# Which queue issues the loads and stores of a spectral layer: tokens to SyncE's queue, the second batch's stores to GpSimd's queue

## The chip, the cores and the metric

The kernel runs on one core of a Trainium2 chip. The metric is the device time of one launch in microseconds (us). The time before is the median of three runs.

## The reference, cut to what matters

The input is an image batch of 2 x 128 x 64 x 64, that is two batches of 4096 positions with 128 channels. It goes through a convolutional attention layer, through a plain self-attention over the positions, and then through the layer that this change is about, a spectral one:

```python
def _stu_conv(phi, u, n):
    sgn = jnp.where(jnp.arange(sl) % 2 == 0, 1.0, -1.0)
    Vf = jnp.fft.rfft(phi, n=n, axis=0)
    Uf_p = jnp.fft.rfft(u, n=n, axis=1)
    Uf_m = jnp.fft.rfft(u * sgn3, n=n, axis=1)
    U_plus = jnp.fft.irfft(Vf[None, :, :, None] * Uf_p[:, :, None, :], n=n, axis=1)[:, :sl]
    U_minus = jnp.fft.irfft(Vf[None, :, :, None] * Uf_m[:, :, None, :], n=n, axis=1)[:, :sl]
    return (U_plus, U_minus * sgn[None, :, None, None])
...
out = jnp.einsum('btkd,k,kde->bte', U_plus, s, Mpp)
out = out + jnp.einsum('btkd,k,kde->bte', U_minus, s, Mpm)
...
return _compute_spectral(u, sigma, phi, Mpp, Mpm) + _compute_ar_u(Mu, u)
```

So 16 causal filters of length 4096 are convolved with every channel, each result is mixed by a 128 x 128 matrix, and a short convolution of three taps (`_compute_ar_u`) is added. The layer's output is added to its own input.

## The kernel before

One launch does everything, in this order: the first attention (lines 193 to 482), the self-attention of batch 0 and then of batch 1 (`attend`, lines 1008 to 1121), and the spectral layer (from line 1274). The program is built by a recording layer that keeps the order of the code on each engine and on each queue.

**What is prepared.** `filters16` writes the transformed filters as "tables" to DRAM. `feed(b)` (lines 1123 to 1212) normalises a batch, transforms it (`pf`, line 1160), splits the result into two float16 parts (`uh`, lines 1132 and 1133) and stores them to DRAM as "rows" (lines 1166, 1167 and 1199). For each of its eight blocks of 512 positions it issues eight stores of 64 KB, in pieces of 256 bytes. Its inner function `taps` computes the three taps plus the layer's input and stores this as "base" (line 1148, 256 KB each), from the single buffer `oc`, which ScalarE writes at line 1140. `feed(0)` runs beside the self-attention of batch 1. `feed(1)` runs beside the first quarter of the spectral layer, as the iterator `beside`.

**The spectral layer's loop.** It runs over batch `b`, output row parity `ro`, eight chunks `ch` and two input streams `s`: 64 steps. In the text a pass is one pair (`b`, `ro`), that is 16 steps, and a half is half a step. For each half, `chunk16` (lines 1300 to 1323) issues two loads of "tokens", 128 KB each, the same rows into partitions 0 to 63 and 64 to 127 (line 1309), and one load of a table, 1024 KB (line 1314). Both kinds of tile have two sets of buffers, so the loads for a half are issued when the convolution of the same half two steps earlier has read its buffers. `convolve16` then multiplies tokens by table on TensorE (`cv`, line 1372; eight matmuls in a half), ScalarE and VectorE split the result into `x` (lines 1379 and 1380), and `mix16` does 48 matmuls for a step (`m`, line 1388).

The two access patterns that matter here, of a token load and of a table load, have different outermost dimensions on the DRAM side: 4 x 16 rows of 2 KB for tokens, 8 x 16 overlapping windows of 8 KB for a table.

`back` (lines 1454 to 1520) turns a finished pass back to positions, four blocks at a time, beside the next pass. `turned` loads the base part of the block into the single buffer `had` (line 1484, 256 KB), and `inverse` adds it (line 1502). After the last pass `back` uses other buffers (`added`, line 1475).

**Queues.** A DMA is issued by an engine, and an engine issues in order: a DMA that waits for data or for a free buffer holds up everything behind it on the same queue. Before the change, SyncE's queue (SP) issues, in the order in which the loop reaches them, the tables of the whole layer, the stores of both feeds, the base stores, the `had` loads, and the four token loads of step 0. GpSimd's queue (POOL) issues the token loads of steps 1 to 63, 252 in all, and has nothing else to do in this stage apart from one memset and some short powers.

Of the kernel before, what the change touches and what calls it, by code (L numbers as in the profile page):

```python
# [38 lines left out]
BP = NI // 2  # L39
# [36 lines left out]
def conv_attn_hybrid(ctx: ExitStack, tc: tile.TileContext, io):  # L76
    nc = tc.nc
# [31 lines left out]
    def pool(stack, name, bufs=1, **kw):  # L109
        return stack.enter_context(tc.tile_pool(name=name, bufs=bufs, reuse_waits="tile", **kw))  # L110
# [599 lines left out]
    base = [dram.tile([C, NI, P], F32, name=f"base{b}") for b in range(B)]  # L710
# [45 lines left out]

    def layers(st, layer0, in_halves):
        psum_a = st.enter_context(ExitStack())

        tokens = [pool(st, f"tok{b}", side="right") for b in range(B)]  # L760
        tok = [tokens[b].tile([P, NI, C], F32, tag="t", name=f"tok{b}") for b in range(B)]
# [360 lines left out]

        def feed(b, p, bank, fw, stats=None):


            if stats is None:
                stats = LayerStats(p, tok[b], f"f{b}")
                yield from stats.steps()
            to = rows16[b].rearrange("h c r w d -> w c h r d") if in_halves else rows[b].rearrange("c r w d -> w c r d")

            def parts(dst, pf):
                nc.scalar.activation(dst[:, 0], pf, AF.Copy, scale=U_SCALE)
                nc.vector.scalar_tensor_tensor(dst[:, 1], pf, U_SCALE, dst[:, 0], ALU.mult, ALU.subtract)

            def taps(i, uT):
                oc = p.tile([P, 4, P], F32, tag="oc", name=f"oc{b}_{i}", bufs=1)
                pt = bank(f"tT{b}_{i}").rearrange("p (t c) -> p t c", c=C)
                for t in range(4):
                    nc.tensor.transpose(pt[:, t, :], tok[b][:, 4 * i + t, :], ident)
                nc.scalar.copy(oc, pt)  # L1140
                yield
                pa = bank(f"ar{b}_{i}").rearrange("p (t c) -> p t c", c=C)
                for n in range(NU):
                    nc.tensor.matmul(pa, mu[:, n, :], uT[:, 2 - n : 6 - n, :], start=(n == 0), stop=(n == NU - 1))  # L1144
                    if n == 0:
                        yield
                nc.vector.tensor_tensor(oc, pa, oc, ALU.add)
                nc.sync.dma_start(base[b][:, 4 * i : 4 * i + 4, :], oc)
                yield

            before = first = None
            for i in range(NQ):
                un = p.tile([P, 4, C], F32, tag="un", name=f"un{b}_{i}")
                for t in range(4):
                    stats.normed(un[:, t, :], 4 * i + t)
                yield
                for c in range(2):
                    at = BP + 1 + 2 * i
                    pf = bank(f"pf{b}_{i}_{c}").rearrange("p (t c) -> p t c", c=C)
                    nc.tensor.matmul(pf, fw[:, c, :], un, start=True, stop=True)  # L1160
                    if in_halves:
                        uh = p.tile([P, 2, 4, C], F16, tag="uh", name=f"uh{b}_{i}_{c}")
                        uhr = uh.rearrange("w h (p r) d -> w h p r d", r=2)
                        parts(uh, pf)
                        for h in range(2):
                            nc.sync.dma_start(to[:, c, h, 2 * i : 2 * i + 2, :], uhr[:, h, :, 0, :])
                            nc.sync.dma_start(to[:, c, h, at : at + 2, :], uhr[:, h, :, 1, :])
                    else:
                        uh = p.tile([P, 4, C], F32, tag="uh", name=f"uh{b}_{i}_{c}")
                        uhr = uh.rearrange("w (p r) d -> w p r d", r=2)  # L1170
                        nc.scalar.copy(uh, pf)
                        nc.sync.dma_start(to[:, c, 2 * i : 2 * i + 2, :], uhr[:, :, 0, :])
                        nc.sync.dma_start(to[:, c, at : at + 2, :], uhr[:, :, 1, :])
                    yield

                uT = p.tile([P, 6, P], F32, tag="uT0" if i == 0 else "uT", name=f"uT{b}_{i}", bufs=1 if i == 0 else 2)
                pt = bank(f"uT{b}_{i}").rearrange("p (t c) -> p t c", c=C)
                for t in range(4):
                    nc.tensor.transpose(pt[:, t, :], un[:, t, :], ident)
                nc.vector.tensor_tensor(uT[:, 2:, :], pt, mask.unsqueeze(1).to_broadcast([P, 4, P]), ALU.mult)  # L1180
                if i:
                    nc.vector.tensor_copy(uT[:, :2, :], before[:, 4:, :])
                    yield
                    yield from taps(i, uT)
                else:
                    first = uT
                    yield
                before = uT
            ul = p.tile([P, 2, 2, C], F16, tag="ul", name=f"ul{b}", bufs=1) if in_halves else p.tile([P, 2, C], F32, tag="ul", name=f"ul{b}", bufs=1)
            for c in range(2):  # L1190
                pf = bank(f"pl{b}_{c}")[:, :C]
                nc.tensor.matmul(pf, fw[:, 2 + c, :], un[:, 3, :], start=True, stop=True)
                if in_halves:
                    parts(ul[:, c], pf)
                else:
                    nc.scalar.copy(ul[:, c, :], pf)
            if in_halves:
                for c in range(2):
                    nc.sync.dma_start(to[:, c, :, BP, :], ul[:, c])
            else:  # L1200
                nc.sync.dma_start(to[:, :, BP, :], ul)
            yield

            nc.gpsimd.memset(first[:, :2, 0:1], 0.0)
            nc.vector.tensor_tensor(
                first[:, :2, 1:],
                before[:, 4:, : P - 1],
                mask[:, 1:].unsqueeze(1).to_broadcast([P, 2, P - 1]),
                ALU.mult,
            )  # L1210
            yield
            yield from taps(0, first)
# [78 lines left out]
        def ordered(instruction):  # L1291
            return tc.keep_in_program_order(instruction)

        def one_bank(name):
            return pc.tile([P, 512], F32, tag="bk", name=name)
# [4 lines left out]
        def chunk16(n, b, ro, ch, s):  # L1300

            row = FIRST[STREAM[ro, s]]
            halves = []
            for half in range(2):
                w0 = 2 * NS * ch + NS * half
                tt = tables_in[n % 2][half]
                ut = tokens_in[n % 2][half]
                for copy in range(2):
                    (nc.gpsimd if n else nc.sync).dma_start(  # L1309
                        ut[64 * copy : 64 * copy + 64],  # L1310
                        rows16[b].rearrange("h c r w d -> (h c) r w d")[:, row : row + BP, w0 : w0 + NS, :],
                    )
                own = tables16[s, w0 // NS]
                nc.sync.dma_start(
                    tt,
                    bass.AP(
                        tensor=own.tensor,
                        offset=own.offset,
                        ap=[[NDI * NS * 2 * NK, 8], [NS * 2 * NK, BP], [1, BP * NS * 2 * NK]],
                    ),  # L1320
                )
                halves.append((tt, ut))
            return halves
# [130 lines left out]
        def back(b, ro, oh, outs, p):  # L1454
# [3 lines left out]
            baser = base[b].rearrange("c (q r) j -> c r q j", r=2)  # L1458
# [18 lines left out]
            def turned(p4):  # L1477

                u = f"{b}_{ro}_{p4}"
                if end:  # L1480
                    had, v = ends[p4][0], ends[p4][1].rearrange("p (c q) x -> p c q x", c=2)
                else:
                    had = p.tile([P, 4, P], F32, tag="had", name=f"had{u}", bufs=1)
                    nc.sync.dma_start(had, baser[:, ro, 4 * p4 : 4 * p4 + 4, :])
                    v = p.tile([P, 2, 4, C], F32, tag="v", name=f"v{u}", bufs=1)
                for c in range(2):
                    pt = pc.tile([P, 512], F32, tag="cv", name=f"vt{u}_{c}", bufs=3) if end else one_bank(f"vt{u}_{c}")
                    pt = pt.rearrange("p (q c) -> p q c", c=C)
                    for q in range(4):
                        ordered(nc.tensor.transpose(pt[:, q, :], ohr[:, c, BP - 1 - 4 * p4 - q, :], ident))  # L1490
                    (nc.scalar.copy if c else nc.vector.tensor_copy)(v[:, c, :, :], pt)
                    yield had, v
# [201 lines left out]
```

## Time and profile before

| what | value |
|---|---|
| time, median of 3 runs | 2817.92 us (2805.27 to 2823.38) |
| the profiled execution | 2826.95 us, of which 2824.8 us are the span of its instructions |
| TensorE busy (PE) | 2686.4 us, 95% of the span |
| VectorE (DVE), ScalarE (ACT), GpSimd (POOL) busy | 1717.3, 1908.9 and 310.7 us |
| spectral layer's loop, first `cv` matmul to last `x` | 1757.9 to 2790.7 us of the span |
| tables, q1 (queue of SP) | 128 loads of 1024 KB |
| tokens, q0 (queue of POOL) | 252 loads of 128 KB, 14.5 us from issue to landing in the median |

How it is read: times in the profile are counted from the start of the span. A row of the view by windows gives a stretch of the span, its length, the busy time of each engine in it with the number of instructions, the mean TensorE clock that was granted (PEclk, 1.00 is full), the mean busy share of the core's 16 DMA engines, and the rate that they moved. A row of the view of waits reads: who waited, for what, how many us in total, how often, and the longest. The chain of waits follows the end of the program back through what released each piece of work. "SPq" and "POOLq" are the queues of SyncE and GpSimd.

### The profile page before, as it was taken

The page shows a single profiled execution, that of the slowest core. Times are in us where ns is not written, and L with a number is a line of the kernel's source. Part 1 is how long each engine was busy: PE and PEld are TensorE (multiplying, and loading weights), DVE is VectorE, ACT ScalarE, POOL GpSimd, SP SyncE. Part 2 cuts the span into 40 slices and gives each one's busy share as a digit, 9 for nine tenths or more (in the row PEclk, how much of TensorE's full clock was granted, in tenths as well). Part 3 has the DMA queues.
Part 4 walks back from the last instruction along what each step waited for, and adds up shares of the span by engine and source line. Part 5 has one row for each costly group of instructions (what it writes and reads, how often), then busy time and mean ns, then how long its engine had stood idle before and what let it go on. Part 6 is the DMA issues. An engine that isn't in the chain of part 4 may idle for free.

```text
span 2824.8 us, 34747 instructions
## 1 busy us (share of the span) xinstructions
PE 2686.4 (95%) x12851; PEld 1365.7 (48%) x12851; DVE 1717.3 (61%) x2994; ACT 1908.9 (68%) x2507; POOL 310.7 (11%) x542
## 2 busy tenths in 40 slices
PE   5999999999999999998899999788989999999998
PEld 3555555555445555554455554343444445445444
DVE  5256564256245249779986677565656666666664
ACT  4999999999999976665555565344444554555553
POOL 2022121013010001000100000111111111111110
PEclk9999999999999999999999999899999999999999
DMA  4122120022000013303121100666666566566662
GB/s 142 34 64 81 49 64 22 5 65 63 6 5 7 5 38 42 59 1 105 38 60 38 36 1 14 141 155 159 169 168 177 192 181 189 174 205 177 164 199 94
DMA packets 215635, 253.31 MB, mean 90 GB/s; under 512 B 140720, under 2 KB 171840, under 8 KB 199072
## 3 DMA queue, kind: packets, MB, share of 16 engines
q1 hardware_dynamic: 168128, 197.35, 24.2%
q0 software_dynamic: 44336, 50.44, 7.8%
q10 hardware_dynamic: 2992, 3.22, 0.3%
q8 instruction: 103, 1.69, 0.3%
q14 instruction: 76, 0.62, 0.1%
HBM read 210.50 MB, written 23.33 MB: 83 GB/s over the span
## 4 chain that ended last, share of the span: by engine, by line
PE 45%; DMA 9%; DVE 7%; ACT 1%; issue 1%; SPq 0%; ACTq 0%; DVEq 0%
PE m L1388 18%; PE oacc L1053 9%; PE cv L1372 6%; DMA tables_b<-tables 5%; PE y L1023 5%; PE eT L1043 3%; DMA base<-oc 2%; PE ar L1144 1%; DMA had<-base 1%; DVE x L1380 1%; DVE ep L1085 1%; PE bk L1500 1%; DVE eT L1046 1%; DMA tables_a<-tables 1%; PE pf L1160 1%
## 5 line engine op out<-in xcount | busy, mean ns | idle before, releaser
L464 ACT ACTIVATE e<-s 128x1536 f16<-128x1536 f32 (+1 forms) x704 | 937.1, 1430 | 33.5 <-PE s L208 28.5
L1380 DVE TENSOR_TENSOR x<-cv,x 128x1024 f16<-128x1024 f32 x512 | 602.8, 1219 | 306.0 <-ACT x L1379 305.9
L1379 ACT CAST x<-cv 128x1024 f16<-128x1024 f32 x512 | 493.7, 1017 | 414.0 <-PE cv L1372 413.1
L1388 PE MATMUL m<-x,mxr 128*128 128x512 f16 x2048 | 624.2, 381 | 0.0
L208 PE MATMUL s<-qs,ks 128*128 128x512 f16 x2048 | 558.3, 380 | 7.5 <-ACT e L464 3.8
L208 PE MATMUL acc<-e,v 128*97 128x512 f16 x2048 | 557.6, 379 | 3.4 <-DVE accs L412 0.2
L1388 PE MATMUL m<-x,mxl 128*128 128x512 f16 x1024 | 392.3, 383 | 3.2 <-DVE oh L1395 3.2
L208 PEld LDWEIGHTS <-v 128*97 128x97 bf16 x2048 | 254.8, 125 | 214.9 <-issue 12.9
L1388 PEld LDWEIGHTS <-mxr 128*128 128x128 f16 x2048 | 201.7, 98 | 244.0 <-issue 7.1
L1032 ACT ACTIVATE ey<-y,nshift 128x512 f32<-128x512 f32 x288 | 195.4, 688 | 179.9 <-PE y L1023 140.5
L208 PEld LDWEIGHTS <-ks 128*128 128x128 f16 x2048 | 200.6, 99 | 228.0 <-issue 44.3
L1309 POOL DMA_DIRECT2D tokens<-rows x252 | 153.0, 611 | 852.0 <-PE cv L1372 819.1
L1023 PE MATMUL y<-bothT 128*128 128x512 f16 x864 | 221.9, 380 | 0.6 <-ACT ey L1032 0.5
L1046 DVE TENSOR_TENSOR eT<-eT,eT 128x512 f16<-128x512 f32 x224 | 147.3, 685 | 93.4 <-ACT eT L1045 91.9
L412 DVE COPY accs<-acc 97x512 f32<-97x512 f32 x64 | 44.2, 691 | 262.2 <-PE acc L208 262.1
L1053 PE MATMUL oacc<-ep,hi 128*128 128x512 f16 x576 | 190.8, 380 | 10.5 <-DVE ep L1085 8.1
L1085 DVE TENSOR_TENSOR ep<-ey,ep 128x512 f16<-128x512 f32 x288 | 192.2, 686 | 6.9 <-ACT ep L1084 0.9
L1372 PEld LDWEIGHTS <-tokens 128*128 128x128 f16 x1024 | 100.4, 99 | 167.4 <-issue 69.9
L1045 ACT ACTIVATE eT<-eT 128x512 f16<-128x512 f32 x224 | 132.6, 602 | 70.1 <-PE eT L1043 69.7
L1388 PEld LDWEIGHTS <-mxl 128*128 128x128 f16 x1024 | 101.1, 99 | 132.8 <-DVE oh L1395 10.6
L1053 PEld LDWEIGHTS <-hi 128*128 128x128 f16 x1024 | 100.5, 98 | 130.2 <-issue 16.8
L1372 PE MATMUL cv<-tables_b,tokens 128*128 128x512 f16 x512 | 135.2, 387 | 23.3 <-DMA tables_b<-tables 21.0
(210 smaller groups left out, 2582.5 us busy)
## 6 DMA issues: line engine op xcount, KB each, us to landing
tables_a<-tables SPq DMA_DIRECT2D x64, 1024.0 KB
tables_b<-tables SPq DMA_DIRECT2D x64, 1024.0 KB
tokens<-rows POOLq DMA_DIRECT2D x252, 128.0 KB, 14.5
tab<-in_rot SPq DMA_DIRECT2D x32, 512.0 KB
rows<-uh SPq DMA_DIRECT2D x128, 64.0 KB
ks<-term POOLq DMA_DIRECT2D x112, 64.0 KB, 2.2
qs<-term POOLq DMA_DIRECT2D x112, 64.0 KB, 2.1
accs<-back SPq DMA_DIRECT2D x32, 128.0 KB
```

The costliest lines, as they stand in the source:

```text
L208: tc.keep_in_program_order(nc.tensor.matmul(*args, **kw))
L464: nc.scalar.activation(e[:, own, :], ps[:, own, :], AF.Exp, scale=SCORE_SCALE)
L1023: nc.tensor.matmul(ps[:, q, :], a[0][:, bass.ts(t, P)], c[0][:, bass.ts(i, 512)], start=(n == 0), stop=(n == 2),)
L1032: nc.scalar.activation(e[:, 2 * h + q, :], ps[:, q, :], AF.Exp, bias=nshift16 if in_halves else nshift, accum_out=den[:, t, i : i + 1],)
L1046: nc.vector.tensor_tensor(eT[1], pt, eT[0], ALU.subtract)
L1053: nc.tensor.matmul(acc, a[0][:, own], c, start=(start and t == 0 and n == 0), stop=(stop and t == len(es) - 1 and n == 2),)
L1085: nc.vector.tensor_tensor(es[t][1], e[:, t, :], es[t][0], ALU.subtract)
L1309: (nc.gpsimd if n else nc.sync).dma_start(ut[64 * copy : 64 * copy + 64], rows16[b].rearrange("h c r w d -> (h c) r w d")[:, row : row + B ...
L1372: ordered(nc.tensor.matmul(pu[:, h, :], ut[:, at, :], tt[:, :, at, :], start=True, stop=True))
L1379: nc.scalar.copy(hi, pur)
L1380: nc.vector.tensor_tensor(lo, pur, hi, ALU.subtract)
L1388: nc.tensor.matmul(acc, m, x, start=(s == 0 and i == 0), stop=(s == 1 and i == len(products) - 1))
```

## The change

The token loads of all steps go to SyncE's queue. The rows and base stores of `feed(1)`, 64 + 2 + 8 in all, and the twelve `had` loads go to GpSimd's queue. `feed(0)` stays on SyncE's queue. The order of the instructions on TensorE, VectorE and ScalarE is the same as before; buffers, sizes and access patterns are the same. After it, SyncE's queue holds in this stage, for each half, two token loads and then one table load, and towards the end the base loads at line 1475 and half of the output.

```diff
@@ def layers
         psum_a = st.enter_context(ExitStack())
+        aside = nc.gpsimd if in_halves else nc.sync
...
@@ def feed(b, p, bank, fw, stats=None)
+            queue = aside if b else nc.sync
...
-                nc.sync.dma_start(base[b][:, 4 * i : 4 * i + 4, :], oc)
+                queue.dma_start(base[b][:, 4 * i : 4 * i + 4, :], oc)
...
-                            nc.sync.dma_start(to[:, c, h, 2 * i : 2 * i + 2, :], uhr[:, h, :, 0, :])
-                            nc.sync.dma_start(to[:, c, h, at : at + 2, :], uhr[:, h, :, 1, :])
+                            queue.dma_start(to[:, c, h, 2 * i : 2 * i + 2, :], uhr[:, h, :, 0, :])
+                            queue.dma_start(to[:, c, h, at : at + 2, :], uhr[:, h, :, 1, :])
...
-                    nc.sync.dma_start(to[:, c, :, BP, :], ul[:, c])
+                    queue.dma_start(to[:, c, :, BP, :], ul[:, c])
...
@@ def chunk16(n, b, ro, ch, s)
-                    (nc.gpsimd if n else nc.sync).dma_start(
+                    nc.sync.dma_start(
                         ut[64 * copy : 64 * copy + 64],
...
@@ def back / turned(p4)
-                    nc.sync.dma_start(had, baser[:, ro, 4 * p4 : 4 * p4 + 4, :])
+                    aside.dma_start(had, baser[:, ro, 4 * p4 : 4 * p4 + 4, :])
```

`in_halves` is true on the path that runs; the same edits in the other path (single precision) are not executed.

## The prediction

> **What bounds the kernel now.** I read the stage first. The spectral loop has four passes of 32 halves. The view by windows, cut where each pass starts its first `cv` matmul, shows where TensorE is short of work. Columns: stretch, length, busy PE, PEld, DVE, ACT and POOL with counts, granted clock, DMA share, GB/s.
>
> ```profile
> 1757.90:2071.30 313.40, 268.24 (x1127) 120.84 (x1125) 187.79 (x219) 137.90 (x157) 39.94 (x65) 0.93 0.63 154
> 2071.30:2310.60 239.30, 233.95 (x1121) 111.85 (x1120) 159.63 (x141) 127.22 (x136) 38.79 (x64) 0.99 0.61 185
> 2310.60:2555.30 244.70, 236.64 (x1124) 112.20 (x1123) 161.01 (x154) 127.43 (x136) 38.78 (x64) 0.99 0.63 186
> 2555.30:2790.70 235.40, 232.39 (x1122) 111.43 (x1121) 160.03 (x141) 127.23 (x136) 33.94 (x56) 1.00 0.57 167
> ```
>
> TensorE bounds passes 2 to 4: 703 of 719.4 us busy. In pass 1, beside which `feed(1)` runs, it idles for 313.4 - 268.2 = 45.2 us, at a clock of 0.93. The chain of waits, in the window of pass 1, says why (start, us, what):
>
> ```profile
> 1757.12 22.75 DMA tables_b<-tables
> ...
> 1792.25 19.03 DMA rows<-uh
> ...
> 1835.26 28.97 DMA tables_b<-tables
> ...
> 1869.71 23.60 DMA base<-oc
> ...
> 1903.62 32.19 DMA tables_b<-tables
> ```
>
> A store of 64 or 256 KB takes as long as a table, because both stand on SP's queue, and tables are issued late behind stores. This is what the change takes away. The queues' shares decide what it costs. The DMA view gives packets, MB and share of 16 engines; these are its q1 (SP) and q0 (POOL) lines for pass 1, passes 2 to 4, and for 2154 to 2300, an even stretch of pass 2:
>
> ```profile
> q1 hardware_dynamic: 23644, 39.98, 49.9%
> ```
>
> ```profile
> q1 hardware_dynamic: 19213, 102.71, 44.3%
> ```
>
> ```profile
> q1 hardware_dynamic: 2911, 22.36, 44.5%
> q0 software_dynamic: 5998, 5.67, 16.1%
> ```
>
> Last, windows of a few us in which one kind of transfer runs. The first three hold the four token loads that SP issues already (issue 1562.5 to 1564.7); the fourth, a base store; the last two, tables alone, with two outstanding:
>
> ```profile
> 1564.00:1566.00 2.00, 2.00 (x12) 0.95 (x10) 1.91 (x4) 1.31 (x5) 0.00 (x0) 1.00 0.22 75
> 1566.00:1568.00 2.00, 2.00 (x7) 0.83 (x7) 1.97 (x4) 0.94 (x2) 0.00 (x0) 1.00 0.26 99
> 1568.00:1569.50 1.50, 1.50 (x9) 0.68 (x8) 0.73 (x2) 0.00 (x0) 0.00 (x0) 1.00 0.26 98
> 1572.90:1573.70 0.80, 0.80 (x7) 0.71 (x6) 0.80 (x7) 0.36 (x1) 0.00 (x0) 1.00 0.84 328
> 1774.00:1776.00 2.00, 0.00 (x0) 0.00 (x0) 0.00 (x0) 0.00 (x0) 0.00 (x0) 0.50 0.50 117
> 1776.00:1778.00 2.00, 0.00 (x0) 0.00 (x0) 0.00 (x0) 0.00 (x0) 0.00 (x0) 0.50 0.49 139
> ```
>
> The share column is the find. A base store keeps nearly all 16 DMA engines busy. Tables never take more than half of them, 8, though a second table is waiting. Token loads issued by SP take a quarter, 4, though four of them are outstanding. The access patterns' outermost DRAM dimensions are 8 and 4. So the stage has a second bound: eight DMA engines that carry all tables, busy nearly all the time.
>
> **The change, part by part.**
>
> *Taken off SP: stores and `had` loads.* The gain is at most pass 1's idle, 45.2 us: then its halves go at TensorE's pace, 268.2 / 32 = 8.4 us instead of 313.4 / 32 = 9.8. The waits of passes 2 to 4 (719.4 - 703 = 16.4 us) could add some of `had`'s 11.9 us (VectorE's wait at line 1502).
>
> *Put on POOL: 66 rows stores, 8 base stores, 12 `had` loads.* POOL takes 0.50 us to issue 32 pieces (`ks`, line 302) and 0.61 us for 64 (line 1309). For 256 pieces a straight line through these gives 1.3 us, a ratio of pieces 2.4 us; I take 1.3. Eight stores in a block cost 10 us, at most 20, and a block lasts about 33 us, so `uh`, with two buffers, isn't late. Behind a waiting store on POOL stand only stores and `had` loads. If the cover failed, `uh` would hold `pf` on TensorE, as once before (3.3 us). The bytes stay. Eight rows stores took 31.7% of 16 engines for 7 us, 4.4 engine-us each; a base store 0.84 x 16 x 0.8 = 10.8. In pass 1 that is 66 x 4.4 + 8 x 10.8 = 377 engine-us, 377 / 16 / 32 = 0.74 us per half on every engine, before and after.
>
> *Taken off POOL: 252 token loads.* 252 x 0.61 = 154 us of an idle engine: nothing. *Put on SP:* 252 x 0.515 us (the four that it issues now) = 130 us, plus 126 tables x 0.575 = 72 us, in 1033 us: covered. In order, two token loads stand ahead of each table, 1 us, against table loads issued two steps ahead.
>
> *What the token loads do to SP's DMA engines* is the term that counts. At 99 GB/s, 131 KB takes 1.32 us: two loads hold four engines for 2.65 us in each half. If these four are none of the tables' eight, this costs nothing. If they are, each half holds those four for a table plus 2.65 us. No row names an engine. But four token loads outstanding stay on four engines, and two tables on eight, so this queue doesn't rotate its choice; I take it that both start from the same engine, the four among the eight.
>
> The Trainium skill, "DMA: Bandwidth & Descriptors", section "Why a DMA increments its semaphore by 16 and not by 1", has a rule against this change: a hardware-issued DMA is spread over the largest number up to 16 that divides the outermost dimensions of both sides, on the lowest-numbered engines, while GpSimd's DMAs go round. The counts of 4 and 8 agree with it; which engines they are, no run here shows. By it the four are among the eight, and the sum would be the one below; by the opposite, the first rival.
>
> *A table's time on its eight engines*, from the q1 lines, with 1.049 MB to a table. In the even stretch: 0.445 x 16 x 146 = 1040 engine-us for 22.36 MB, so 48.8 a table, 6.1 us on each of eight. Passes 2 to 4: 0.443 x 16 x 719.4 = 5099 for 102.71 MB, 6.5 us. Pass 1: 0.499 x 16 x 313.4 = 2502, less 377 for 6.4 MB of stores: 2125 for 33.6 MB, 8.3 us. A quiet window (2525 to 2540: 43.9%, 2.51 MB): 5.5 us. Packets of tables are thus slower at some times than at others, and I can't derive when. I take 6.1, the row with a second table always waiting and no stores; against the slower rows speaks that the other four engines will now idle a quarter of the time, so fewer read at once.
>
> *Sum.* A half takes the longer of TensorE's work and of the four engines':
> - Passes 2 to 4: 6.1 + 2.65 = 8.75 us, above TensorE's 703 / 96 = 7.3. 96 x 8.75 = 840, against 719.4: +120 us.
> - Pass 1: 6.1 + 2.65 + 0.74 = 9.5 us, above 8.4. Two halves are loaded beforehand; the first wait for a table, 22 us, stays. 30 x 9.5 + 22 = 307, against 313.4: -6 us.
>
> Together +114 us on the profiled execution's own 2826.95 us, 2941 us. That execution is 9 us above the median of the runs; from the median the forecast is 2932 us. The wait moves from SP's stores to the matmuls at line 1372. TensorE then idles 1.4 us a half in passes 2 to 4; after idle its granted clock fell (0.50 from 1774 to 1778). That is covered while its half stays under 8.75 us, to a mean clock of 7.3 / 8.75 = 0.83.
>
> Bounds. A table at 5.5: passes 2 to 4 96 x 8.15 = 782 (+63), pass 1 30 x 8.9 + 22 = 289 (-24): +39, 2857 us. At 6.5 and, in pass 1, 8.3: 96 x 9.15 = 878 (+159), 30 x 11.7 + 22 = 373 (+60): +219, 3037 us. At 8.3 throughout: 96 x 10.95 = 1051 (+332), +60: 3210 us.
>
> **Rivals.**
> 1. *Faster: the tokens' four engines are none of the eight, or have room.* Then only the first part counts: -45 us, minus the first wait for a table, which is not SP's doing (12.7 us): about -33, with `had`'s waits up to -45; 2773 to 2785 us. For it: SP's queue is the visible cause in pass 1. Against it: the fixed choice of engines. It decides if a table's time plus 2.65 is under 7.3, that is under 4.65 us; no row is that low. Chance 0.14.
> 2. *Gain and loss cancel.* A table at 5.3 us or less, so 7.95 x 96 = 763 (+44) and pass 1 at 8.7 x 30 + 22 = 283 (-30): +14, 2832 us. For it: the quiet window; against it: 6.5 as the mean over three passes. Chance 0.11.
> 3. *Much slower: tables stay at pass 1's pace*, 8.3 us, in all passes: 3210 us; a half-way case, 7.2 throughout, gives 96 x 9.85 + 340 = 1286 against 1032.8, 3071 us. For it: pass 1 itself, and that two kinds of transfers now alternate in each half. Chance above 3090 us: 0.09.
> 4. *The stores don't leave the tables' way*, since they share the engines: that is the 0.74 us, already counted.
>
> **How the numbers follow.** Forecast 2932 us: token loads on the tables' engines, slower, within 2857 to 3090 us, chance 0.66. With rival 3's 0.09, slower by over 1% has 0.75 (1%, 28 us, is about what a measurement of this kernel can tell from no change), within 1% 0.11, faster 0.14. The range reaches from 2795, which cuts off most of rival 1, to 3090, which cuts off the slow part of rival 3; its ends leave about 0.2 outside.
>
> **What would show it.** Right: in passes 2 to 4 TensorE waits at line 1372 for tables or tokens in nearly every half, its busy share there falls to 80 to 90%, halves are 8 to 9.5 us apart; the DMA share falls below 0.6, with stretches at 0.25 to 0.3, where only tokens run; token loads land later than the 14.5 us of now. Waits for `base<-oc` and `rows<-uh` are gone in pass 1. Wrong: passes 2 to 4 still take 240 us each and pass 1 shrinks towards 268 us; then the four engines are others. Wrong in size: the q1 engine-us per MB in passes 2 to 4 leave 42 to 52.

## The result, and the profile after

The changed kernel takes 3129.67 us in the median of four runs (3114.1 to 3154.81), against 2811.6 us (2800.91 to 2823.38) for the kernel before: a ratio of 1.113, with a 95% interval of 1.1085 to 1.1177. The prediction said 2932 us, within 2795 to 3090. The direction was right, and so was the place where the time is lost, but the size was far too small: some 318 us were lost, not 114.

The view by windows of the changed kernel, cut again where each pass starts its first `cv` matmul (columns as in the prediction: stretch, length, busy PE, PEld, DVE, ACT, POOL, granted clock, DMA share, GB/s; the last row stops a little before the end of pass 4):

```profile
1756.10:2089.70 333.60, 275.56 (x1127) 121.92 (x1126) 188.32 (x219) 138.21 (x157) 53.87 (x76) 0.93 0.51 144
2089.70:2421.40 331.70, 256.40 (x1120) 114.50 (x1120) 159.97 (x140) 127.78 (x136) 3.00 (x4) 0.94 0.48 130
2421.40:2754.10 332.70, 261.24 (x1124) 116.19 (x1125) 161.09 (x153) 127.72 (x136) 2.99 (x4) 0.92 0.49 136
2754.10:3079.60 325.50, 260.74 (x1107) 115.39 (x1108) 157.63 (x138) 125.85 (x134) 2.24 (x3) 0.91 0.46 125
```

All four passes now take the same time, 332 / 32 = 10.4 us a half, whether or not the second batch's stores run beside them. Before, pass 1 took 313 us and the others 235 to 245. So nearly the whole loss, about 90 us in each, lies in passes 2 to 4. TensorE is busy for 77 to 80% of them; its wait is in the view of waits of its engine from 2089.7 to 3079.6 (who waits, for what, us in total, times, longest):

```profile
PE cv L1375 <- DMA tables_a<-tables: 104.6, 39, 4.9
PE cv L1375 <- DMA tables_b<-tables: 95.1, 37, 4.6
PE cv L1375 <- DMA tokens<-rows: 12.2, 8, 3.2
```

That is 84 waits in 96 halves, almost all for a table. What stands between one table and the next is in the chain of waits between 2600 and 2700 (start, us, what):

```profile
2609.44 23.00 DMA tables_a<-tables
...
2632.46 6.77 SPq L1312
...
2639.27 23.24 DMA tables_b<-tables
...
2662.53 5.59 SPq L1312
...
2668.17 23.36 DMA tables_b<-tables
```

Tables of 23 us follow each other through SP's queue, and between them SP spends 5.6 to 6.8 us on issuing token loads at line 1312. The prediction counted 0.515 us for one such issue, the price of the four that SP issued before, and called them covered. The view of line 1312 has the shortest, median and longest in ns, first for the changed kernel, then for experiment 10 below, which has the same number of loads in the same order:

```profile
L1312 SPq DMA_DIRECT2D tokens<-rows x256: 514/1316/9704, 1560.8 to 3046.3; - x128
```

```profile
L1312 SPq DMA_DIRECT2D tokens<-rows x256: 574/574/814, 1449.1 to 2702.9; - x128
```

In passes 2 to 4 the 184 token loads took 3.49 us each in the mean to issue, 642 us of 990, and the 93 tables 2.03 us each. So SP's issuing was held up, and the next table was issued late. Experiment 10 shows that the number of loads is not what held it up.

The share of the DMA engines (tenths, in 40 slices of the same 100 us, and the line of SP's queue) tells where the pieces lie:

```profile
DMA  3555355545424543454435443544454345534545
...
q1 hardware_dynamic: 2762, 13.30, 46.7%
```

No digit is above 5, and SP's share is 46.7%. With two token loads and one table load to a half on one queue, SP's transfers used no more than about half of the 16 engines: the token loads did not go to others than the tables' eight.

### The profile page after: what moved, and what is told of

The parts are those of the page before. It is cut to its first block, busy times and chain, and to the rows that moved or that the text cites. A ratio compares the mean times of both kernels' runs of the same rounds, so it can differ in the third digit from the quotient of the medians.

```text
span 3116.1 us, 34633 instructions
## 1 busy us (share of the span) xinstructions
PE 2771.8 (89%) x12851; PEld 1378.3 (44%) x12851; DVE 1717.9 (55%) x2994; ACT 1910.5 (61%) x2507; POOL 218.9 (7%) x376
## 4 chain that ended last, share of the span: by engine, by line
DMA 34%; PE 19%; SPq 7%; DVE 4%; ACT 1%; issue 1%; ACTq 0%; DVEq 0%
DMA tables_b<-tables 16%; DMA tables_a<-tables 15%; PE oacc L1054 9%; SPq L1312 7%; PE y L1024 4%; DMA tokens<-rows 3%; PE eT L1044 3%; PE m L1391 1%; DVE ep L1086 1%; PE ar L1147 1%; DVE eT L1047 1%; DVE pm L751 1%; ACT ey L1033 1%; PE pf L1163 0%; PE cv L1375 0%
## 5 line engine op out<-in xcount | busy, mean ns | idle before, releaser
L1391 PE MATMUL m<-x,mxr 128*128 128x512 f16 x2048 | 657.6, 398 | 0.0
L1391 PE MATMUL m<-x,mxl 128*128 128x512 f16 x1024 | 427.0, 417 | 0.0
L1391 PEld LDWEIGHTS <-mxr 128*128 128x128 f16 x2048 | 210.3, 103 | 274.4 <-issue 58.2
L1375 PE MATMUL cv<-tables_a,tokens 128*128 128x512 f16 x512 | 145.7, 410 | 137.4 <-DMA tables_a<-tables 119.3
L1375 PE MATMUL cv<-tables_b,tokens 128*128 128x512 f16 x512 | 143.2, 405 | 131.4 <-DMA tables_b<-tables 126.8
L1054 PE MATMUL oacc<-ep,hi 128*128 128x512 f16 x576 | 191.0, 380 | 10.4 <-DVE ep L1086 7.9
L1391 PEld LDWEIGHTS <-mxl 128*128 128x128 f16 x1024 | 108.7, 106 | 148.5 <-issue 48.0
```

Source lines behind the costliest of these rows:

```text
L1054: nc.tensor.matmul(acc, a[0][:, own], c, start=(start and t == 0 and n == 0), stop=(stop and t == len(es) - 1 and n == 2),)
L1375: ordered(nc.tensor.matmul(pu[:, h, :], ut[:, at, :], tt[:, :, at, :], start=True, stop=True))
L1391: nc.tensor.matmul(acc, m, x, start=(s == 0 and i == 0), stop=(s == 1 and i == len(products) - 1))
```

## The experiments

The line numbers are those of the changed kernel. A pass is 32 halves; "a half" below is the time of a pass divided by 32.

**1. Only the token loads move.** The stores, the base and the `had` loads stay on SP's queue.

```diff
 # kernel before
-                    (nc.gpsimd if n else nc.sync).dma_start(
+                    nc.sync.dma_start(
                         ut[64 * copy : 64 * copy + 64],
```

> Only the token loads go to SyncE's queue; stores, base parts and had loads stay there as before. Theory A (token loads issued by SyncE sit on four of the eight DMA engines that carry the tables, and these four set the pace): as slow as the whole change or a little slower, since the stores' way through SyncE's queue comes back in pass 1: 3120 to 3180 us. Theory B (the order on SyncE's queue sets the pace: three loads in line in each half, each waiting for the one ahead): the same, with the stores in line too, 3150 to 3250 us. If the loss came from the stores on GpSimd's queue, it would be at 2810.

Measured: 3162.1 us (3157.36 to 3165.82), ratio 1.1245 (1.1188 to 1.1302). Passes 1 to 4 take 359.7, 343.3, 340.1 and 326.2 us. The whole loss is in this part. This fits theories A and B alike; experiment 4 separates them. The rest of the change, done on top of it, is worth 3129.7 - 3162.1 = -32 us.

**2. Only the stores, the base and the `had` loads move.** The token loads stay on POOL's queue, behind them.

```diff
 # changed kernel
-                    nc.sync.dma_start(
+                    (nc.gpsimd if n else nc.sync).dma_start(
                         ut[64 * copy : 64 * copy + 64],
```

> Only the second batch's stores, base parts and had loads go to GpSimd's queue, behind the token loads that stay there. Theories A and B: the loss is gone; pass 1 gains some of its 45 us of TensorE idle, 2765 to 2805 us. If the stores on GpSimd's queue cost something, 2830 or more.

Measured: 2869.33 us in the median of six runs that spread from 2840 to 2902, ratio 1.0204 (1.0143 to 1.0265): 1 to 3% slower, where a gain was expected. In the profiled execution, which is the fastest of the six, pass 1 did gain 11 us (302.1 for 313.4), but pass 2 lost 18 (257.3 for 239.3). The trace of POOL's queue there shows an instruction with what it waited for in brackets, and the next one:

```profile
2121.82 0.80 POOL L1487 DMA_DIRECT2D had<-base  x1 [24.13 <-DVE out L1505]
2122.62 1.25 POOL L1312 DMA_DIRECT2D tokens<-rows  x2
```

A `had` load waits 24 us until VectorE has read the single buffer `had`, and the next token loads stand behind it. TensorE's waits in this pass, though, are 12.8 us for VectorE, which itself waited for a `had` load (16.5 us at the longest), and only 0.8 us for tokens. The next experiment takes the `had` loads away.

**3. As 2, but the `had` loads stay on SP's queue.**

```diff
 # kernel of experiment 2
-                    aside.dma_start(had, baser[:, ro, 4 * p4 : 4 * p4 + 4, :])
+                    nc.sync.dma_start(had, baser[:, ro, 4 * p4 : 4 * p4 + 4, :])
```

> Only the rows and base stores of the second batch go to GpSimd's queue; the had loads stay on SyncE's queue and the token loads on GpSimd's. Theory E (in the run with both, token loads stood on GpSimd's queue behind had loads that waited for their buffer, up to 24 us): passes 2 and 4 lose nothing now, pass 1 keeps what it gained, 2790 to 2825 us, at least 1% below the run with both. If the stores themselves cost the 2%: again 2850 to 2880 us.

Measured: 2817.71 us, ratio 0.9986 (0.9949 to 1.0023). So what experiment 2 lost came with the `had` loads on POOL's queue. That it came from the token loads behind them is not shown: here too pass 2 takes 247.2 us, and TensorE waits 11.4 us in it for VectorE, which waits 15.1 us for one `had` load. The stores alone bring nothing while the token loads share their queue: pass 1 takes 304.0 us, 9 less than before, but pass 2 takes 8 more.

**4. The whole change, with token loads over 16 engines.** The rows lie in DRAM with the image row outermost, so that a token load is one dimension of 64 rows and no longer 4 x 16. The partitions of the tokens then don't pair with those of the tables, so the convolution multiplies other rows; pieces, bytes and order are the same.

```diff
 # changed kernel
-    rows16 = [dram.tile([2, 2, DROWS, NF, C], F16, ...) for b in range(B)]
+    rows16 = [dram.tile([DROWS, 2, 2, NF, C], F16, ...) for b in range(B)]
...
-                        rows16[b].rearrange("h c r w d -> (h c) r w d")[:, row : row + BP, w0 : w0 + NS, :],
+                        rows16[b].rearrange("r h c w d -> (r h c) w d")[4 * row : 4 * row + 4 * BP, w0 : w0 + NS, :],
```

> The whole change, with the rows laid out in DRAM so that the 64 rows of a token load are one dimension of 64 instead of 4 x 16. Number, size, queue and order of all DMAs stay the same; the tokens' partitions then stand in an order that doesn't match the tables', so that part of the computation is changed. Theory A: a token load spreads over 16 engines, 0.33 us each instead of 1.32 us on four, so a half takes 6.1 to 7.5 us on the tables' engines and the loop falls back to TensorE's pace: 2770 to 2850 us. Theory B: nothing changes on SyncE's queue, 3100 to 3150 us.

Measured: 2768.68 us (2765.63 to 2770.72), ratio 0.9844 (0.9794 to 0.9894). Passes 274.8, 232.8, 233.2 and 233.2 us. The window of pass 2, and the queue's line for passes 2 to 4:

```profile
2034.50:2267.40 232.90, 232.28 (x1122) 111.60 (x1121) 159.99 (x141) 127.21 (x136) 3.00 (x4) 1.00 0.58 188
```

```profile
q1 hardware_dynamic: 27844, 123.46, 53.7%
```

In passes 2 to 4 TensorE hardly waits any more, and SP's share is above half. The order on the queues is that of the changed kernel, so order is not what cost 318 us.

**5. The whole change, with one token load in a half.** From step 2 on only partitions 0 to 63 are loaded; the upper ones keep old rows.

```diff
-                for copy in range(2):
+                for copy in range(2 if n < 2 else 1):
```

> The whole change, with one token load in a half instead of two from step 2 on; the second copy of the rows in partitions 64 to 127 is left out (they hold those of steps 0 and 1). Theory A: a half loses half of the tokens' time on the four engines, between 1.3 us (at the rate of four lone token loads) and 1.9 us (half of what is left of a half after a table of 6.6 us): 126 x 1.3 to 1.9 = 165 to 240 us less, 2890 to 2965 us. Theory B: two loads in line instead of three, a third off the excess over TensorE's pace: about 3020 us.

Measured: 2823.78 us, ratio 0.9985 (0.9929 to 1.0041); passes 271.0, 240.0, 259.8 and 263.2. That is below both ranges. One load of the two costs 306 us in 124 halves, 2.5 us each, more than its 1.32 us alone.

**6. No token loads at all, and a third of the mixing matmuls.** From step 2 on no tokens are loaded, and `mix16` keeps only one of its three products, so that TensorE does not hide the tables' pace.

```diff
-                for copy in range(2):
+                for copy in range(2 if n < 2 else 0):
...
-            products = [(m[:, k, s, :], xh[:, k, :]) for k in range(NK) for m in (mxl, mxr)]
-            products += [(mxr[:, k, s, :], xl[:, k, :]) for k in range(NK)]
+            products = [(mxr[:, k, s, :], xh[:, k, :]) for k in range(NK)]
```

> The whole change, without token loads from step 2 on, and with a third of the mixing matmuls (first parts alone), so that TensorE needs some 3.5 us a half and VectorE 4.9. What is left to set the pace are the tables on their eight engines. Theory A with the forecast's price: 6.1 us a half. If tables alone run at the fastest packets seen, 5.0 us; if the slow rows of pass 1 are a property of the tables themselves, 8.3 us.

Measured: 2591.59 us. Pass 2, and TensorE's waits in it:

```profile
1963.70:2149.90 186.20, 144.08 (x608) 62.73 (x608) 154.84 (x141) 129.37 (x137) 3.00 (x4) 0.94 0.52 186
```

```profile
PE cv L1375 <- DVE x L1383: 39.4, 69, 1.3
...
PE cv L1375 <- DMA tables_a<-tables: 0.7, 1, 0.7
```

186.2 / 32 = 5.8 us a half, and TensorE waits for VectorE, not for tables. So in pass 2 tables alone take at most 5.8 us on their eight engines. Passes 1, 3 and 4 take 205.2, 223.8 and 190.6 us, and pass 3, at 7.0 us a half, is another matter. From 2149.9 to 2373.7 TensorE waits 31.5 us for tables, most of them in this stretch, shown by its window and the line of SP's queue:

```profile
2220.00:2300.00 80.00, 44.43 (x150) 15.89 (x148) 45.03 (x40) 37.21 (x39) 0.00 (x0) 0.79 0.51 122
```

```profile
q1 hardware_dynamic: 1275, 9.62, 50.7%
```

There are no token loads in it and hardly any other transfers. The tables keep half of the engines busy all the time and still get only 9.62 MB through in 80 us, about 9 us a table. So tables alone have a fast pace and a slow one, and what decides between them the run does not show. Over passes 2 to 4 a half takes 600.6 / 96 = 6.3 us.

**7. The same cut in the mixing, with two token loads and with one.** Both are the changed kernel with the cut of experiment 6; the second has also the edit of experiment 5.

> The whole change, all loads, with a third of the mixing matmuls. Theory A: the pace is that of four DMA engines, and TensorE's work doesn't count: a half stays at 10.4 us in passes 2 to 4, the launch at 3060 to 3130 us. If TensorE's work or its clock had a part in the loss, halves fall to 8 or 9 us.

> The whole change with one token load in a half (from step 2 on) and a third of the mixing matmuls. Without tokens a half took at most 5.8 us in pass 2 and with two loads 10.8. If each token load adds the same, 8.3 us; if the second load costs more than the first (the clash grows with the tokens' share), 7 to 7.5 us.

Measured with two: 3171.28 us, passes 351.3, 345.4, 348.2 and 341.7, which is 10.7 to 11.0 a half. With one: 2806.17 us, passes 266.5, 247.5, 260.7 and 248.1, or 7.7 to 8.3. With two thirds of the mixing gone the time doesn't fall (it lies 41 us above the range, in a single run): TensorE's work, and its lower clock, set nothing in the changed kernel. The window of pass 2 with two loads has the clock at 0.70 and TensorE busy for about half of it:

```profile
2109.40:2454.80 345.40, 178.19 (x609) 70.33 (x610) 157.96 (x140) 127.28 (x136) 3.00 (x4) 0.70 0.48 125
```

**8. The kernel before, with the same cut.**

> The kernel before with a third of the mixing matmuls: how near its own DMA engines were to setting the pace. From the 6.1 to 6.5 us a half that its tables took in passes 2 to 4: 6.2 to 7 us a half, just under TensorE's 7.3, so that the kernel before had almost no room.

Measured: 2826.69 us, beside 2823.7 us for the kernel before on the same chip; passes 280.1, 248.0, 242.2 and 271.3, or 7.6 to 8.8 a half. TensorE's waits from 2070 to 2790:

```profile
PE cv L1372 <- DVE x L1380: 86.7, 111, 3.4
PE cv L1372 <- DMA tables_a<-tables: 57.3, 17, 9.7
PE cv L1372 <- DMA tables_b<-tables: 42.1, 13, 6.7
PE cv L1372 <- DMA tokens<-rows: 37.2, 11, 7.1
```

With two thirds of the mixing gone, the kernel before is no faster. The halves are longer than the 6.2 to 7 us expected. TensorE waits for VectorE, which allowed 5.8 us a half in pass 2 of experiment 6, and longer, 136.6 us in sum, for loads. Passes 2 to 4 of the kernel before were bound by TensorE, at 95% busy and more, and very nearly by the loads as well: there was no room behind TensorE.

**9. Is it where the token pieces lie in DRAM?** Here the token loads of the changed kernel read 4 x 16 pieces of 2 KB that lie almost side by side; the rows read are other ones (`BP` is 16).

```diff
-                        rows16[b].rearrange("h c r w d -> (h c) r w d")[:, row : row + BP, w0 : w0 + NS, :],
+                        bass.AP(tensor=rows16[b].tensor, offset=rows16[b].offset + (2 * ch + half) * 70 * NS * C,
+                                ap=[[17 * NS * C, 4], [NS * C, BP], [1, NS * C]]),
```

> The whole change, but each token load reads a nearly contiguous stretch of the rows (4 x 16 pieces of 2 KB, 16 in a row, then a gap of 2 KB) instead of 64 pieces that lie 32 KB or more apart; the data are other rows, so that part of the computation is changed. Pieces, bytes, number of DMA engines, queue and order are the same. The question is why a pair of token loads costs a half some 4.6 us beside tables when it takes 2.65 us alone. Theory C (the spread-out DRAM addresses clash with the tables' reads): the pair falls back to about 2.7 us, a half to 8.5, the launch to 2870 to 2900 us. Theory D (what counts is that short and long pieces alternate on the same engines, wherever they are read): no change, 3100 to 3150 us.

Measured: 3149.45 us, ratio 1.1148 (1.1058 to 1.1238). Pass 2 takes 341.8 us. That the pieces lie far apart is not the cause.

**10. The same pieces in eight groups.** This is experiment 9 with another grouping: 64 pieces of 2 KB again, but 8 x 8.

```diff
 # kernel of experiment 9
-                                ap=[[17 * NS * C, 4], [NS * C, BP], [1, NS * C]]),
+                                ap=[[9 * NS * C, 8], [NS * C, 8], [1, NS * C]]),
```

> The whole change, with the token loads reading eight groups of eight pieces of 2 KB instead of four groups of sixteen (other rows' data; as many pieces and bytes), so that the outermost size is 8. Theory A (a pair of token loads occupies four of the tables' engines, and costs them 4.6 to 5 us a half beside the tables): on all eight of the tables' engines the same pieces cost each of them half of that, 2.3 to 2.5 us; with the 5.8 us that the tables took alone a half is 8.1 to 8.3 us, passes 2 to 4 take 259 to 266 us each, and the kernel some 2830 to 2870 us. Rival F (a token load costs a fixed time per transfer beside the tables, a start or an end on the queue, whatever engines it takes): a half stays at 10.4 us, the passes at 330 to 342 us and the kernel at 3130 to 3150 us.

Measured: 2774.88 us (2768.55 to 2781.2), ratio 0.9827 (0.9734 to 0.9919). Passes 275.0, 232.8, 233.2 and 233.2. Pass 2, and SP's queue from 2050 to 2740:

```profile
2033.80:2266.60 232.80, 232.18 (x1121) 111.50 (x1120) 159.88 (x141) 127.20 (x136) 3.01 (x4) 1.00 0.52 185
```

```profile
q1 hardware_dynamic: 27917, 121.68, 48.7%
```

The fixed time per transfer falls. So does the size that the other theory gave: a half was to take 8.1 to 8.3 us and takes 232.8 / 32 = 7.28, TensorE's own pace. This is the sharpest pair of the study. Experiments 9 and 10 move the same number of pieces and bytes, on the same queue in the same order, and in both SP's mean share stays below half; with the pieces on four of the tables' eight the kernel takes 3149 us, with the pieces on all eight 2775.

**11. Tokens and tables over 16 engines.** The rows as in experiment 4, and each table load in two parts of 64 partitions whose outermost dimension is 16 instead of 8, so that tokens and tables pair again. Once with the queues of the changed kernel, once with those of the kernel before.

```diff
-                nc.sync.dma_start(tt, ... ap=[[NDI * NS * 2 * NK, 8], [NS * 2 * NK, BP], [1, BP * NS * 2 * NK]])
+                for h in range(2):
+                    nc.sync.dma_start(tt[64 * h : 64 * h + 64], ... offset=own.offset + h * 4 * NDI * NS * 2 * NK,
+                        ap=[[NS * 2 * NK, BP], [NDI * NS * 2 * NK, 4], [1, BP * NS * 2 * NK]])
```

> The whole change, with rows laid out so that a token load is one dimension of 64, and with each table loaded in two parts of 512 KB whose outermost dimension is 16, in the partition order that fits these tokens. Theory A (the loads' number of DMA engines sets the pace): tables too spread over 16 engines, 3 to 4 us a half instead of 6 to 8; TensorE sets the pace everywhere, 2730 to 2770 us, at or a little below the 2768 us of the run that spread the tokens alone. Theory B (the order and number of loads on SyncE's queue): four loads in a half instead of three, no better than 3100 us.

> The kernel before, queues as they were, with the same layout of rows and tables as in spread16. Theory A: the tables leave room, so the stores on SyncE's queue no longer wait for slow tables and pass 1 loses most of its 45 us of idle: 2750 to 2790 us, within 1% of spread16: then the queue of the stores hardly matters once the tables are spread. Theory B: as the kernel before, 2800 to 2830 us, or slower by the one load more in a half.

Measured with the changed queues: 2752.81 us (2751.32 to 2752.98), ratio 0.9757 (0.9724 to 0.9789). With the queues as before: 2752.18 us (2749.89 to 2754.63), ratio 0.9759 (0.9726 to 0.9791). In both, the passes take 260.6, 232.8, 233.2 and 233.2 us. Passes 1 and 2 of the first:

```profile
1757.80:2018.40 260.60, 254.01 (x1127) 118.58 (x1126) 187.42 (x219) 137.57 (x157) 53.87 (x76) 1.00 0.78 191
2018.40:2251.20 232.80, 232.18 (x1121) 111.50 (x1120) 159.88 (x141) 127.21 (x136) 3.00 (x4) 1.00 0.77 185
```

This beats both kernels, by 2.4% the one before. The clock is full, and TensorE is busy for 97% and more. Which queue issues the loads and stores, the whole subject of the change, then makes no difference that can be measured.

## Why the prediction was right and wrong

**Right: the term that counts.** The prediction said that two token loads, issued by SP, sit on four of the tables' eight DMA engines and set the pace of every half. Experiment 1 shows that the loss belongs to the token loads alone, experiment 4 that it goes when they spread over 16 engines, and experiment 10 that four against eight engines decides. TensorE waits in most halves, its busy share fell to 77 to 80%, a little below the 80 to 90% named, and the chain runs through tables and SP's issuing of token loads. The first rival (other engines, or room on these) is out, and so is the second.

One reading behind this was wrong. The windows from 1774 to 1778 were taken for tables alone on eight engines, but POOL's queue was at work in them too; from 1774 to 1780:

```profile
q1 hardware_dynamic: 81, 0.60, 39.7%
q0 software_dynamic: 80, 0.17, 11.0%
```

That tables stay on eight engines is shown by experiment 6, where they have SP's queue to themselves and its share is 50.7% in the slow stretch, with 49.1% in pass 2.

The rule that the prediction weighed, in the Trainium skill, "DMA: Bandwidth & Descriptors", section "Why a DMA increments its semaphore by 16 and not by 1", takes the number of engines of a hardware-issued DMA from the outermost dimensions of both sides, and puts them on the lowest-numbered engines. The runs agree with the counts of 4, 8 and 16: a share of 0.26 for the loads of 4 x 16, half for tables of 8 x 16, 0.77 for the layout with 16. Which numbers the engines have, no run shows. That the smaller sets lie inside the larger one, which the prediction could only assume, is now shown by the share that stays below half, and by the loss itself.

**Right about the waits, luck in the size: the stores' move.** The waits for `base<-oc` and `rows<-uh` are gone from pass 1, where TensorE (the same view of waits, 1756.1 to 2089.7) now waits for tables, as shown below. Experiment 1 and the whole change differ by 32 us, close to the 33 us that the prediction gave for this part. But it gave them for the case that TensorE sets the pace, which did not come about, and by experiment 3 the stores' move alone is worth nothing.

```profile
PE cv L1375 <- DMA tables_b<-tables: 31.7, 10, 10.4
PE cv L1375 <- DMA tables_a<-tables: 19.6, 7, 4.9
```

**Wrong in size: the issue on POOL, harmlessly.** A rows store of 256 pieces was put at 1.3 us. The trace of the changed kernel has 0.72 us in the median of 32 (0.71 to 0.78), hardly more than the 0.61 us for 64 pieces: the straight line through the counts of 32 and 64 didn't go on.

**Wrong: the price of the token pair, 2.65 us.** This is the step that failed. It was read from windows in which SP's four token loads ran alone, and added to a table's 6.1 us as if one did not disturb the other, with their issue on SP taken as covered. On the profiled executions the sum said 2941 us and 3118.3 was measured, 177 more. Passes 2 to 4 took 331.7 + 332.7 + 328.9 = 993 us (pass 4 to the end of its last `x`) instead of 840, which is 153 of these, and pass 1 took 333.6 instead of 307, 27 more; the stretches around the loop gave back some 3.

A half of passes 2 to 4 took 10.4 us instead of 8.75. The packet records say how these are made up. A pair of token loads puts 32 pieces of 2 KB on each of four engines, and a table puts 16 pieces of 8 KB on each of eight. In passes 2 to 4 a token piece took 118 ns in the mean, so a pair takes 3.8 us and not 2.65. For at least 99% of the time four or more of SP's packets are in flight there, so the four engines hardly ever rest, and 10.4 - 3.8 = 6.6 us are left for their part of a table, not 6.1. This split is an estimate: it takes the four engines that never rest to be the four with the tokens, and the records name no engine. By differences of whole runs the pair costs more: experiment 6 allowed 5.8 us a half in pass 2 without token loads and 6.3 over passes 2 to 4, so that the pair costs 4.1 to 4.6 us. Whichever way it is counted, most of what the sum lacked is in the price of the pair, and the table's term was nearly right.

Why company makes it dearer, the runs narrow down but do not show. It is not the distance of the pieces in DRAM (experiment 9), and not the mere turn of short and long pieces on an engine, which experiment 10 has on all eight. There a token piece took 97 ns and a table piece 354; 16 of each make 7.2 us, and the half takes 7.28. In the changed kernel table pieces took 476 ns in the mean over all eight engines, and only 30% of them under 335 ns, against 69% in experiment 10. Token loads on half of the tables' engines are thus one thing that goes with slow table pieces, but not the only one. Without any token loads table pieces took 361 ns in pass 2 of experiment 6 and 558 in the slow stretch of its pass 3, and in pass 1 of the kernel before they took 505. Nor are slow pieces a loss by themselves: in experiment 11, over 16 engines, they took 571. The held-up issue on SP is a second candidate, since the next table then comes late to all eight engines. It may as well follow from the full four, and no experiment separates the two. So the cause of the higher price stays open.

The prediction named a sign for an error in size, the time of SP's queue per MB. SP's queue took 0.456 x 16 x 990 us = 7223 engine-us for 124.56 MB from 2089.7 to 3079.6, which is 58 per MB and not 42 to 52.

```profile
q1 hardware_dynamic: 25918, 124.56, 45.6%
```

**Wrong in form: stretches at a quarter of the engines.** The prediction expected stretches at 0.25 to 0.3 in which only tokens run. The packet records show moments with exactly four of SP's packets in flight, 11% of the time in passes 2 to 4 of the changed kernel against 1% in experiment 10. But nearly all of them are shorter than 0.5 us, so that a window of 2 us doesn't show them as such, and on average only 1.2 of the four packets are token pieces. The late engines are working off pieces of tables as well.

**Half right: "TensorE bounds passes 2 to 4".** It did, 703 of 719 us, but this hid a second bound close behind: experiment 8, with much less for TensorE to do, is no faster. The prediction did name the eight engines as second bound. What it lacked was that their load, with tokens issued by POOL, already left almost no time, so that nearly every microsecond added would show.

**The third rival was nearer than the forecast.** Its half-way case, 3071 us, is nearest to the result. It took tables at 7.2 us throughout, between the pace of passes 2 to 4 and that of pass 1, for the reason that two kinds of transfers now alternate. Table pieces did become slow, 476 ns in passes 2 to 4 where they had taken 400 before, and nearly as slow as the 505 of pass 1. But the alternation is not the reason, by experiment 10, and the rival left the pair at 2.65 us.

## What to carry to other kernels

Before a load is moved to another engine's queue, count the DMA engines that it will use there: here the queue of SyncE took 4, 8 or 16 by the outermost dimensions of the access pattern, and the smaller sets lay inside the larger ones, so loads with small outermost dimensions pile up on engines that other loads need. Reshaping the pattern (4 x 16 to 8 x 8 or to 64) was worth 350 us and more against the changed kernel, in experiments that read other rows; with tokens and tables over 16 engines and the right rows it was 377 us, and which queue issues the loads and stores was then worth nothing. A price read from a window in which a transfer runs alone can be too low: 2.65 us for the pair became 3.8 to 4.6 beside tables. And an engine at 95% busy doesn't tell that nothing else is at its limit.

## What had not been expected of the hardware

Equal bytes in equal pieces on one queue made 2775 or 3149 us, depending on whether token loads took all of the tables' eight DMA engines or four of them. Eight engines that carried nothing but tables (experiment 6) had two paces, 5.8 us a table or less and about 9. And full use is not needed: with tokens and tables on eight engines only, at a share of 0.52, passes 2 to 4 were as fast (232.8 to 233.2 us) as with 16 engines at 0.77.
